# Attention over an image: the SBUF tiles of the main path moved to multiples of 128 bytes

## The chip, the cores and the metric

The kernel runs on one core of a Trainium2 chip. The metric is the device time of one execution in microseconds (us). Several executions are timed and the median is given. A profile of one execution shows when each instruction of each engine started: PE is TensorE's matmuls, PEld its weight loads, DVE is VectorE, ACT is ScalarE, POOL is GpSimd and SP is SyncE. SBUF is the on-chip memory that all of them read. A tile is a piece of it: 128 partitions, and in each partition a run of bytes at the same address. The address of a tile below is its byte address in the partition.

## The reference

For each of 4 images of 64 x 64 positions with 256 channels, with N = 4096:

```python
q = jnp.einsum('bwhc,cd->bwhd', x, Wq) + bq      # 256 -> 128
k = jnp.einsum('bwhc,cd->bwhd', x, Wk) + bk      # 256 -> 128
v = jnp.einsum('bwhc,cd->bwhd', x, Wv) + bv      # 256 -> 256
pq, pk, pv = (t.reshape(B, -1, N) for t in (q, k, v))
energy = jnp.einsum('bcn,bcm->bnm', pq, pk)
attention = jax.nn.softmax(energy, axis=-1)
out = jnp.einsum('bcm,bnm->bcn', pv, attention).reshape(B, W, H, C)
return gamma * out + x
```

All of it is float32. The energies are 4096 x 4096 for each image, with an inner dimension of 128; the second large product takes them with v.

## The kernel before

Both large products are done in `float32r`, a form of float32[...]. To keep the accuracy, each operand is split: a high part `h` of few bits, and two combinations `l` and `d` with the rest; three products, h with h, l with l and d with d, are put together to one. So there are three tiles of v that stay for an image (`vh`, `vl`, `vd`), three of the exponentials (`h`, `l`, `d`), and three forms in each `q` and `k` tile. `vh` and `vl` have two more columns, of ones: their product gives the sum of a softmax row.

The loop goes over groups of 256 columns n (16 in an image, `NG`) and in each over units of 512 m (8 in a group, `NU`). A unit has 12 energy matmuls and 24 attention matmuls:

```python
def energy(b, u, k):                                   # twice per unit, k = 0, 1
    ...
    for i in range(2):
        for to, f, first, last in ((sa, 0, True, False), (sa, 1, False, True), (sb, 2, True, True)):
            nc.tensor.matmul(
                to[:, i], kt[:, 2 * k + i, f, :], q[:, :, f, :], start=first, stop=last
            )
    ...                                                # two exponentials on ScalarE

def attend(b, u, j):                                   # twice per unit, j = 0, 1
    ...
    for out_, left, right in ((a, h, vh), (a, l, vl), (bb[:, j, :], d, vd)):
        for i in range(4):
            m = 2 * t + i // 2 + NI * (i % 2)
            nc.tensor.matmul(
                out_, left[:, i, n], right[:, m, :], ...
            )
```

The first operand, of 128 x 128, is the stationary one: it is loaded into TensorE by a weight load. The second is the moving one: it is streamed, 256 columns in the energies (two runs of 128) and in `bb`, 258 in `a`. So every matmul reads two pieces of SBUF, 512 bytes of each partition for the weights and 1024 or 1032 for the columns.

The tiles come from pools, which lie one behind the other; what is allocated first has the lowest address:

```python
    zall = const.tile([P, B * NG, NJ], F32, name="zall")
    bv4_sb = const.tile([P, KC], F32, name="bv4_sb")
    ...
        xpool, xtpool, qkv = pool("xpool", 3), pool("xtpool", 3), pool("qkv", 1)
        ppool, work, kpool = pool("ppool", 2), pool("work", 2), pool("kpool", 3)
    ...
        vh = qkv.tile([P, NM, C + 2], F32R, tag="vh", name="vh")
        vl = qkv.tile([P, NM, C + 2], F32R, tag="vl", name="vl")
        vd = qkv.tile([P, NM, C], F32R, tag="vd", name="vd")
```

`xpool` holds the tiles of x, `xtpool` the transposed ones (`xts`), `ppool` the exponentials (`x`, `y`, `h`, `l`, `d`), `work` the tiles `qks`, `v4`, `qr`, `q`, `o`, `r`, and `kpool` `f` and `k`. For each group, `load_q` fetches `qr`, `halve_q` makes the three forms `q` of it two units later, and at the group's end ScalarE copies `bb` into `o`, from which the result is made in steps during the next units (a reciprocal `r`, a scaling, four transposes, a sum with x and a store). At the very end the row sums in `zall` are tested (`ok`, `zs`, a matmul `zp`), and a second, general path is taken where they are out of range; with these inputs it isn't.

Of the kernel before, what the change touches and what calls it, by code (L numbers as in the profile page):

```python
# [9 lines left out]
F32 = mybir.dt.float32  # L10
F32R = mybir.dt.float32r
I32 = mybir.dt.int32
AF = mybir.ActivationFunctionType
ALU = mybir.AluOpType
AX = mybir.AxisListType
# [5 lines left out]
def kernel(  # L21
# [36 lines left out]
    nc = tc.nc  # L58
    B, W, H, C = x.shape
    P = 128  # L60
    N = W * H
    C2 = C // 2
    NM = N // P
    KC = C // P
    NI = NM // 2
    Z_LOW, Z_HIGH = 2.0**-60, 2.0**80
# [11 lines left out]
    const = ctx.enter_context(tc.tile_pool(name="const", bufs=1))  # L78
# [8 lines left out]
    ones = const.tile([P, P], F32, name="ones")  # L87
# [87 lines left out]
    NJ = NB // P  # L175
    NG = N // NB
    NU = NM // 4
    STEPS = NG * NU
    LOOK = 3
    E = 2.0**-12  # L180


# [4 lines left out]
    zall = const.tile([P, B * NG, NJ], F32, name="zall")  # L187
    bv4_sb = const.tile([P, KC], F32, name="bv4_sb")
    nc.scalar.mul(bv4_sb, bv_sb, 1.0 / E)

    with ExitStack() as fast:
        fast.enter_context(tc.manual_schedule())
# [3 lines left out]
        xpool, xtpool, qkv = pool("xpool", 3), pool("xtpool", 3), pool("qkv", 1)  # L196
        ppool, work, kpool = pool("ppool", 2), pool("work", 2), pool("kpool", 3)
# [3 lines left out]
        ps_t = pool("ps_t", 1, space=PSUM)  # L201


        vh = qkv.tile([P, NM, C + 2], F32R, tag="vh", name="vh")
        vl = qkv.tile([P, NM, C + 2], F32R, tag="vl", name="vl")
        vd = qkv.tile([P, NM, C], F32R, tag="vd", name="vd")
        for t in (vh, vl):
            nc.vector.tensor_copy(t[:, :, C:], ones[:, : 2 * NM].rearrange("p (m t) -> p m t", t=2))

        images, qd, kf, units, loads, now = [], {}, {}, {}, {}, {}  # L210

# [13 lines left out]
        def image(b):  # L225
# [7 lines left out]
            def v_out(i):  # L233
                now["v4"] = work.tile([P, KC, C], F32, tag="v4", name=f"v4_{b}_{i}")
                return now["v4"], bv4_sb, 1.0 / E

# [7 lines left out]
        def halved(f, x):  # L244

            h = f[:, :, 0, :]
            nc.scalar.activation(h, x, AF.Identity, scale=UPPER / 64)  # L247
            for j, s, op in ((1, -64.0, ALU.add), (2, 64.0 * (1.0 + E), ALU.subtract)):
                nc.vector.scalar_tensor_tensor(
# [12 lines left out]
        def project_v(b, i):  # L262
# [3 lines left out]
            h = vh[:, m, :C]  # L266
            nc.scalar.activation(h, v4, AF.Identity, scale=UPPER * E)  # L267

            for t, f in ((vl, 1.0 / E), (vd, 1.0 / E + 1.0)):
                nc.vector.scalar_tensor_tensor(  # L270
# [1 line left out]
                )  # L272

        def load_q(b, g):
            t = work.tile([P, NJ, P], F32, tag="qr", name=f"qr_{b}_{g}")
            nc.sync.dma_start(t, qd[b, g])
            loads[b, "qr", g] = t

# [11 lines left out]
        def energy(b, u, k):  # L290
# [10 lines left out]
# [5 lines that stand above are left out]
            for to, sp, scale in ((x, sa, (1.0 + E) / E), (y, sb, -1.0 / E)):  # L306
                nc.scalar.activation(  # L307
# [28 lines left out]
        def attend(b, u, j):  # L336
            g, t = divmod(u, NU)
            if t == j == 0:
                now["acc"] = [
                    ps_o.tile([P, C + 2], F32, tag=f"a{j}", name=f"a{j}_{b}_{g}")  # L340
                    for j in range(NJ)
                ]
                now["bb"] = ps_o.tile([P, NJ, C], F32, tag="bb", name=f"bb_{b}_{g}")
            h, l, d = units[b, u]
            a, bb = now["acc"][j], now["bb"]
            n = slice(j * P, (j + 1) * P)
# [4 lines that stand above are left out]
                    nc.tensor.matmul(  # L351
                        out_,
                        left[:, i, n],
                        right[:, m, :],
                        start=(t == i == 0 and (left is h or left is d and j == 0)),
                        stop=(t == NU - 1 and i == 3 and left is not h),
                        skip_group_check=True,
                    )
            if t == NU - 1 and j == NJ - 1:
                now["o"] = work.tile([P, NJ, C], F32, tag="o", name=f"o_{b}_{g}")  # L360
                nc.scalar.copy(now["o"], bb)

        def whole(b, g):
# [10 lines left out]

        def finish(b, g, o, xr):
            yield
            r = work.tile([P, NJ], F32, tag="r", name=f"r_{b}_{g}")
            nc.vector.reciprocal(r, zall[:, b * NG + g, :])
            nc.vector.tensor_tensor(r, r, gam.to_broadcast([P, NJ]), ALU.mult)  # L379
            for j in range(NJ):  # L380
                nc.scalar.activation(  # L381
                    o[:, j, :], o[:, j, :], AF.Identity, scale=r[:, j : j + 1]
                )
            yield
            yield
            tp = ps_t.tile([P, 2, NB], F32, tag="t", name=f"ot_{b}_{g}")
            for s in range(2):
                for j in range(NJ):
                    nc.tensor.transpose(  # L389
                        tp[:, s, j * P : (j + 1) * P], o[:, j, s * P : (s + 1) * P], ident  # L390
                    )
            yield
            nc.vector.tensor_tensor(xr, xr, tp, ALU.add)
            nc.gpsimd.dma_start(ov[b, g], xr)

        def begin(b, i):

            if i == 8:
                load_q(b, 0)
            if i == 9:  # L400
                halve_q(b, 0)
            if 8 <= i <= 10:
                load_k(b, i - 8)
            if i >= 10:
                energy(b, (i - 10) // 2, i % 2)
            if i in (12, 14):
                join(b, i // 2 - 6)
            if i in (13, 15):
                upper(b, i // 2 - 6)
                load_k(b, i // 2 - 3)  # L410

        image(0)
        for b in range(B):
# [17 lines left out]
            for u in range(STEPS):  # L431
                g, t = divmod(u, NU)
                ahead = u + LOOK
                if ahead // NU + 1 < NG and ahead % NU == 3:
                    load_q(b, ahead // NU + 1)
# [22 lines left out]
                for j in range(NJ):  # L458
                    attend(b, u, j)
                if t == NU - 1:  # L460
                    whole(b, g)
                    start(finish(b, g, now["o"], loads.pop((b, "x", g))))
# [5 lines left out]
                proceed()  # L468


    zs = const.tile([P, 1], F32, name="zs")
    zf = zall.rearrange("p n j -> p (n j)")
    ok = const.tile([P, B * NG * NJ], F32, name="ok")
    nc.vector.tensor_scalar(ok, zf, Z_LOW, None, ALU.is_ge)
    nc.vector.scalar_tensor_tensor(ok, zf, Z_HIGH, ok, ALU.is_le, ALU.mult)
    nc.vector.tensor_reduce(zs, ok, AX.X, ALU.min)
    nc.vector.tensor_scalar(zs, zs, 0.5, None, ALU.is_lt)
    with tc.tile_pool(name="ps_z", bufs=1, space=PSUM) as ps_z:
        zp = ps_z.tile([P, 1], F32, name="zp")
# [4 lines left out]
    NG = N // NB  # L484
    NJ = NB // P
    NP = NM // 2
    xg, og = columns(x, NB), columns(out, NB)
    with tc.If(nc.values_load(again[0:1, 0:1]) > 0), ExitStack() as general:
# [3 lines left out]
        xpool, xtpool, qkv = pool("gx", 2), pool("gxt", 2), pool("gqkv", 1)  # L492
        ppool, work = pool("gp", NP + 2), pool("gw", 1)
# [3 lines left out]
        for b in range(B):  # L497
# [16 lines left out]
            for g in range(NG):  # L514
                ps = []
                mx = work.tile([P, 2, NB], F32, tag="mx", name=f"gmx_{b}_{g}")
                for t in range(NP):
# [9 lines left out]
                    p = ppool.tile([P, 2, NB], F32, tag="p", name=f"gp_{b}_{g}_{t}")  # L527
# [52 lines left out]
                r = work.tile([P, NB], F32, tag="r", name=f"gr_{b}_{g}")  # L580
# [36 lines left out]
```

## Time and profile before

| | |
|---|---|
| median of 3 runs | 2519.22 us (2517.83 to 2520.44) |
| span of the profiled execution | 2518.5 us |
| mean granted TensorE clock | 0.998 |
| VectorE in a stretch of 400 us of the main loop (600 to 1000) | 332.91 us busy |
| ScalarE in the same stretch | 286.26 us busy |
| bytes moved | 498.92 MB, mean 198 GB/s |

The page counts the busy time of each engine; a busy time is a union, so instructions that overlap count once. Matmuls are pipelined: one lasts longer than the distance to the next, and the distance of their starts is what a matmul costs in a row of them. In the list of groups a line gives the source line, the engine, the output and the inputs by the program's names, the shape, the number of instructions, then busy us and the mean ns of one, then the time that the engine was idle just before them. In the timeline a line is a row of like instructions: start, duration of the whole row, and their number behind the x.

### The profile page before, as it was taken

To read this page: it belongs to the slowest core of one execution; us is meant where nothing else is said; L and a number is where in the kernel's file an instruction comes from. 1 tells how busy PE (TensorE), PEld (TensorE's weight loads), DVE (VectorE), ACT (ScalarE), POOL (GpSimd) and SP (SyncE) were. 2 spreads that over 40 slices of the span, in tenths; PEclk is the share of its full clock that TensorE was granted. 3 is DMA by queue.
4 is the path that set the end of the run, shared out by engine and by line. 5 is a ranking of instruction groups with operands and counts; after the bars stand their busy time and mean duration, and the time that the engine had idled before them with its cause. 6 is when DMAs were issued, how large, how long until landed. Compare 5 with 4: busy or idle time off the path is not lost.

```text
span 2518.5 us, 49987 instructions
## 1 busy us (share of the span) xinstructions
PE 2486.5 (99%) x19970; PEld 2440.1 (97%) x19970; DVE 2103.0 (84%) x2440; ACT 1806.3 (72%) x3138; POOL 425.3 (17%) x774
## 2 busy tenths in 40 slices
PE   8999999999999999999999999999999999999998
PEld 7999999999899999999989999999998999999998
DVE  5888888888688888888868888888886888888887
ACT  5777777777677777777667777777766777777775
POOL 3211111111411111111041111111114111111110
PEclk9999999999999999999999999999999999999999
DMA  6666666665766666666476666666647666666663
GB/s 220 204 207 206 199 200 194 211 196 156 230 214 190 209 202 201 206 192 203 139 236 210 196 200 208 198 205 197 192 144 243 209 207 192 204 200 206 199 196 101
DMA packets 137967, 498.92 MB, mean 198 GB/s; under 512 B 15872, under 2 KB 57856, under 8 KB 137728
## 3 DMA queue, kind: packets, MB, share of 16 engines
q0 software_dynamic: 92160, 453.03, 57.0%
q1 hardware_dynamic: 44032, 41.96, 5.5%
q8 instruction: 160, 2.62, 0.4%
q10 hardware_dynamic: 1536, 0.66, 0.1%
q14 instruction: 79, 0.65, 0.1%
HBM read 445.25 MB, written 50.33 MB: 197 GB/s over the span
## 4 chain that ended last, share of the span: by engine, by line
PE 91%; issue 3%; ACT 3%; DVE 2%; DMA 1%; POOL 0%; POOLq 0%; ACTq 0%; DVEq 0%
PE a L351 38%; PE bb L351 19%; PE sa L303 18%; PE sb L303 10%; PE qk L136 2%; PE v L157 2%; PE ot L389 1%; ACT v L166 1%; DMA k<-kf 1%; ACT vh L267 1%; DVE qks L145 1%; PE xt L123 0%; ACT f L247 0%; DVE vd L270 0%; DVE x L317 0%
## 5 line engine op out<-in xcount | busy, mean ns | idle before, releaser
L307 ACT ACTIVATE x<-sa 128x512 f32<-128x512 f32 x1024 | 608.8, 595 | 431.3 <-PE sa L303 422.3
L317 DVE TENSOR_TENSOR x<-x,y 128x1024 f32<-128x1024 f32 x512 | 625.1, 1221 | 165.6 <-ACT y L307 165.6
L303 PE MATMUL sa<-q,k 128*128 128x256 f32 x4096 | 744.8, 280 | 8.8 <-DMA k<-kf 4.8
L351 PE MATMUL a<-vh,h 128*128 128x258 f32 x4096 | 666.8, 285 | 0.0
L351 PE MATMUL a<-vl,l 128*128 128x258 f32 x4096 | 659.5, 283 | 1.7 <-DVE l L328 1.7
L351 PE MATMUL bb<-vd,d 128*128 128x256 f32 x4096 | 650.7, 281 | 1.8 <-DVE d L331 1.8
L303 PEld LDWEIGHTS sa<-q,k 128*128 128x128 f32 x4096 | 622.9, 188 | 10.8 <-ACT x L307 5.0
L328 DVE TENSOR_TENSOR l<-x,h 128x1024 fp32r<-128x1024 f32 x512 | 623.2, 1217 | 0.0
L331 DVE SCALAR_TENSOR_TENSOR d<-h,x 128x1024 fp32r<-128x1024 f32 x512 | 623.1, 1217 | 0.0
L307 ACT ACTIVATE y<-sb 128x512 f32<-128x512 f32 x1024 | 612.9, 599 | 0.0
L303 PE MATMUL sb<-q,k 128*128 128x256 f32 x2048 | 576.3, 281 | 0.0
L351 PEld LDWEIGHTS a<-vl,l 128*128 128x128 f32 x4096 | 563.0, 189 | 2.6 <-DVE l L328 2.6
L322 ACT ACTIVATE h<-x 128x1024 fp32r<-128x1024 f32 x512 | 543.3, 1061 | 29.1 <-DVE x L317 29.1
L351 PEld LDWEIGHTS a<-vh,h 128*128 128x128 f32 x4096 | 560.6, 190 | 1.1
L351 PEld LDWEIGHTS bb<-vd,d 128*128 128x128 f32 x4096 | 556.4, 188 | 2.6 <-issue 2.0
L287 POOL DMA_DIRECT2D k<-kf x512 | 283.6, 554 | 1487.3 <-PE sb L303 1470.5
L303 PEld LDWEIGHTS sb<-q,k 128*128 128x128 f32 x2048 | 384.5, 188 | 8.9 <-ACT y L307 1.0
L136 PE MATMUL qk<-wqk_sb,xts 128*128 128x256 f32 x512 | 124.5, 387 | 3.5 <-ACT xts L129 3.5
L157 PE MATMUL v<-xts,wv_sb 128*128 128x256 f32 x512 | 120.3, 379 | 0.0
L381 ACT ACTIVATE o<-o,r 128x256 f32<-128x256 f32 x128 | 58.3, 503 | 73.9 <-DVE r L379 73.9
L157 PEld LDWEIGHTS v<-xts,wv_sb 128*128 128x128 f32 x512 | 97.4, 190 | 13.3
L136 PEld LDWEIGHTS qk<-wqk_sb,xts 128*128 128x128 f32 x512 | 94.5, 194 | 14.7 <-ACT xts L129 3.9
(41 smaller groups left out, 876.2 us busy)
## 6 DMA issues: line engine op xcount, KB each, us to landing
k<-kf POOLq DMA_DIRECT2D x512, 768.0 KB, 4.8
x<-in_x_dram SPq DMA_DIRECT2D x128, 256.0 KB, 3.4
kf<-f POOLq DMA_DIRECT2D x64, 384.0 KB, 3.5
out_dram<-x POOLq DMA_DIRECT2D x64, 256.0 KB, 2.5
qd<-qks POOLq DMA_DIRECT2D x128, 64.0 KB, 2.2
qr<-qd SPq DMA_DIRECT2D x64, 128.0 KB, 3.1
wv_sb<-in_L_conv_Wv_dram ACTq DMA_DIRECT2D x1, 256.0 KB, 4.3
wqk_sb<-in_L_conv_Wq_dram ACTq DMA_DIRECT2D x1, 128.0 KB, 2.1
```

Of the source, the lines that this page charges most:

```text
L136: nc.tensor.matmul(qk[:, s, :], self.xt[i][:, k, s, :], wqk_sb[:, k, :], start=(k == 0), stop=(k == KC - 1),)
L145: nc.vector.tensor_tensor(dst, qk[:, :, o : o + w], bqk_sb[:, o : o + w].unsqueeze(1).to_broadcast([P, 2, w]), ALU.add,)
L157: nc.tensor.matmul(vp[:, eh, :], wv_sb[:, k, eh * P : (eh + 1) * P], self.xt[i][:, k].rearrange("p s a -> p (s a)"), start=(k == 0), stop= ...
L287: nc.gpsimd.dma_start(t.rearrange("p (i s) f d -> p i s (f d)", s=2), kf[b, u % NU])
L303: nc.tensor.matmul(to[:, i], kt[:, 2 * k + i, f, :], q[:, :, f, :], start=first, stop=last)
L307: nc.scalar.activation(to[:, 2 * k : 2 * k + 2, :], sp.rearrange("p i j d -> p i (j d)"), AF.Exp, scale=scale,)
L317: nc.vector.tensor_tensor(x, x, y, ALU.mult)
L322: nc.scalar.activation(h, units[b, u], AF.Identity, scale=UPPER)
L328: nc.vector.tensor_tensor(l, x, h.bitcast(F32), ALU.subtract)
L331: nc.vector.scalar_tensor_tensor(d, h.bitcast(F32), 1.0 + E, x, ALU.mult, ALU.subtract)
L351: nc.tensor.matmul(out_, left[:, i, n], right[:, m, :], start=(t == i == 0 and (left is h or left is d and j == 0)), stop=(t == NU - 1 and ...
L381: nc.scalar.activation(o[:, j, :], o[:, j, :], AF.Identity, scale=r[:, j : j + 1])
```

## The change

It places the tiles of the main path at addresses that are multiples of 128 bytes, and the rows of `vh` and `vl` 272 floats (1088 bytes) apart instead of 258 (1032 bytes). A filler tile of 64 bytes at the end of the constants moves what comes after it; small tiles whose size isn't a multiple of 128 bytes (`r`, `zs`, `ok`) leave the pools of the main path. The wider rows need more memory, so `qr` and `o` have one buffer instead of two. The matmuls read the same numbers of columns as before.

```diff
+    VC = C + 16
+    PAD = 16
...
+    zs = const.tile([P, 1], F32, name="zs")
+    rs = const.tile([P, 2, NJ], F32, name="rs")
+
+    const.tile([P, PAD], F32, name="pad")
...
-        vh = qkv.tile([P, NM, C + 2], F32R, tag="vh", name="vh")
-        vl = qkv.tile([P, NM, C + 2], F32R, tag="vl", name="vl")
+        vh = qkv.tile([P, NM, VC], F32R, tag="vh", name="vh")
+        vl = qkv.tile([P, NM, VC], F32R, tag="vl", name="vl")
         vd = qkv.tile([P, NM, C], F32R, tag="vd", name="vd")
         for t in (vh, vl):
-            nc.vector.tensor_copy(t[:, :, C:], ones[:, : 2 * NM].rearrange("p (m t) -> p m t", t=2))
+            nc.vector.tensor_copy(t[:, :, C : C + 2], ones[:, : 2 * NM].rearrange("p (m t) -> p m t", t=2))
...
-            t = work.tile([P, NJ, P], F32, tag="qr", name=f"qr_{b}_{g}")
+            t = work.tile([P, NJ, P], F32, tag="qr", name=f"qr_{b}_{g}", bufs=1)
...
-                        right[:, m, :],
+                        right[:, m, : out_.shape[1]],
...
-                now["o"] = work.tile([P, NJ, C], F32, tag="o", name=f"o_{b}_{g}")
+                now["o"] = work.tile([P, NJ, C], F32, tag="o", name=f"o_{b}_{g}", bufs=1)
...
-            r = work.tile([P, NJ], F32, tag="r", name=f"r_{b}_{g}")
+            r = rs[:, g % 2, :]
...
-    zs = const.tile([P, 1], F32, name="zs")
     zf = zall.rearrange("p n j -> p (n j)")
-    ok = const.tile([P, B * NG * NJ], F32, name="ok")
-    nc.vector.tensor_scalar(ok, zf, Z_LOW, None, ALU.is_ge)
...
+    with tc.tile_pool(name="check", bufs=1) as check:
+        ok = check.tile([P, B * NG * NJ], F32, name="ok")
+        nc.vector.tensor_scalar(ok, zf, Z_LOW, None, ALU.is_ge)
...
```

The addresses that the two builds assign, as the remainder by 128:

| tile | before | after |
|---|---|---|
| `ident`, `wqk_sb`, `wv_sb` | 0 | 0 |
| `x`, `xts`, `q`, `qr`, `o`, `qks`, `v4`, `x`, `y`, `h`, `l`, `d`, base of `vh`, `vl`, `vd` | 32 | 0 |
| `k`, `f` | 96 | 0 |
| rows of `vh`, `vl` | 32, 40, 48, ... (all 16 multiples of 8) | 0 and 64 in turn |
| rows of `vd` | 32 | 0 |

More of the change, by code (lines that the diff above doesn't have):

```diff
@@ L468 @@
                 proceed()
-    zs = const.tile([P, 1], F32, name="zs")
     zf = zall.rearrange("p n j -> p (n j)")
-    ok = const.tile([P, B * NG * NJ], F32, name="ok")
-    nc.vector.tensor_scalar(ok, zf, Z_LOW, None, ALU.is_ge)
-    nc.vector.scalar_tensor_tensor(ok, zf, Z_HIGH, ok, ALU.is_le, ALU.mult)
-    nc.vector.tensor_reduce(zs, ok, AX.X, ALU.min)
+    with tc.tile_pool(name="check", bufs=1) as check:
+        ok = check.tile([P, B * NG * NJ], F32, name="ok")
+        nc.vector.tensor_scalar(ok, zf, Z_LOW, None, ALU.is_ge)
+        nc.vector.scalar_tensor_tensor(ok, zf, Z_HIGH, ok, ALU.is_le, ALU.mult)
+        nc.vector.tensor_reduce(zs, ok, AX.X, ALU.min)
     nc.vector.tensor_scalar(zs, zs, 0.5, None, ALU.is_lt)
```

## The prediction

> **What bounds the kernel now.** I read four views in this order: the busy shares, the chain of work that ended last, the costliest groups, and then short stretches of the timeline of TensorE, because the first three only say which engine it is and not what sets its pace.
>
> ```profile
> PE 2486.5 (99%) x19970; PEld 2440.1 (97%) x19970; DVE 2103.0 (84%) x2440; ACT 1806.3 (72%) x3138; POOL 425.3 (17%) x774
> PEclk9999999999999999999999999999999999999999
> PE 91%; issue 3%; ACT 3%; DVE 2%; DMA 1%; POOL 0%; POOLq 0%; ACTq 0%; DVEq 0%
> L303 PE MATMUL sa<-q,k 128*128 128x256 f32 x4096 | 744.8, 280 | 8.8 <-DMA k<-kf 4.8
> L351 PE MATMUL a<-vl,l 128*128 128x258 f32 x4096 | 659.5, 283 | 1.7 <-DVE l L328 1.7
> L351 PE MATMUL bb<-vd,d 128*128 128x256 f32 x4096 | 650.7, 281 | 1.8 <-DVE d L331 1.8
> L303 PEld LDWEIGHTS sa<-q,k 128*128 128x128 f32 x4096 | 622.9, 188 | 10.8 <-ACT x L307 5.0
> ```
>
> The reader is to see three things: TensorE is busy 99% at a full clock, it carries 91% of the last chain, and its three big groups waited only 8.8, 1.7 and 1.8 us in the whole run. So nothing that feeds TensorE matters; only the pace of its own matmuls does. The means of 280 to 283 ns are lengths of overlapping instructions, not the pace. The pace is the distance between starts:
>
> ```profile
> 21.78 0.60 PE L123 MATMUL xt<-ident,x 128*128 128x128 f32 x4
> 22.22 0.60 PE L136 MATMUL qk<-wqk_sb,xts 128*128 128x256 f32 x2
> ...
> 1004.06 0.39 PE L303 MATMUL sa<-q,k 128*128 128x256 f32 x2
> 1004.29 0.28 PE L303 MATMUL sb<-q,k 128*128 128x256 f32 x1
> 1004.40 0.39 PE L303 MATMUL sa<-q,k 128*128 128x256 f32 x2
> 1004.63 0.28 PE L303 MATMUL sb<-q,k 128*128 128x256 f32 x1
> 1004.74 0.64 PE L351 MATMUL a<-vh,h 128*128 128x258 f32 x4
> 1005.22 0.64 PE L351 MATMUL a<-vl,l 128*128 128x258 f32 x4
> 1005.69 0.28 PE L351 MATMUL bb<-vd,d 128*128 128x256 f32 x1
> ```
>
> The first column is the start in us. Three energy matmuls go from 1004.06 to 1004.40, 113 ns each; four attention matmuls from 1004.74 to 1005.22, 120 ns each, though they stream nearly the same number of columns. The four transposes, whose cost is nearly all weight load, take 110 ns each (21.78 to 22.22). Taking the start-to-start distance of every record between 100 and 140 ns (longer ones are waits), the whole trace has: energies (6144) mean 115.3; attention `a` (8192, 258 columns) mean 120.6; attention `bb` (4096, 256 columns) mean 118.0; transposes 109.2.
>
> **What the Trainium skill says.** Its page "TensorE: Matmul & The Clock Gate", section "Back-to-back issue gap", gives N/2.4 + 2.5 ns between warm matmuls: 109.2 ns for 256 columns, 110.0 for 258. This trace reaches that only where nothing competes at the full rate: the fp32 projection runs at 216 ns for 256 columns at two cycles each (512/2.4 + 2.5 = 215.8), while the 18432 fp32r matmuls are 6 to 10 ns above it. The section "LDWEIGHTS (loading the stationary operand)" gives 128/1.2 = 106.7 ns; the transposes at 109.2 agree. So in the main loop weight load and matmul are equally long, and any hiccup of either is paid. The section "Step-by-step: what each phase is for" says that the two read SBUF through independent ports, so that a load steals nothing from the running matmul. The trace does not bear this out: each alone would give 109 or 110, together they give 113 to 120. Last, "SBUF — State Buffer", section "Door 1: The DMA port swizzle", has 16-byte lines, a crossing costing extra. It says nothing of 64 or 128 bytes.
>
> **The change part by part.** The instruction sequence of every engine is the same in both builds, but for names and one pair at the very end. What moves are addresses. In the build of before all the streamed and stationary tiles (`x`, `xts`, `q`, `h`, `l`, `d`, the bases of `vh`, `vl`, `vd`) begin 32 bytes past a multiple of 128, `k` and `f` 96 past; rows of `vh` and `vl` are 1032 bytes, so each begins 8 bytes further round than the last, and every odd row is only 8-aligned. In the new build all these begin on 0 of 128, and rows of `vh`, `vl` (1088 bytes) alternate between 0 and 64.
>
> *Rows.* The old kernel measures part of this by itself, as its rows pass through all sixteen positions. `a` from `vh`: even rows (16-byte aligned) 119.9 and 119.4 ns for `vh` and `vl`, odd rows 121.9 and 121.0. `bb`, whose rows are all alike, has 117.5 and 118.5 at the same places, so 1.0 of that is the place in the loop. What an 8-byte start costs is about 0.8 ns on 4096 matmuls: 3 us. And rows that already begin on 0 of 128 run at 119.8 (`vh`) and 119.3 (`vl`), no better than those at 16, 32 or 48. Alignment of the moving rows alone is thus worth almost nothing while the stationary tiles lie 32 bytes off.
>
> *Stationary tiles and q.* Here the old kernel gives no contrast, since all its fp32r weights are 32 off a multiple of 64. The excess over the floor of each kind is what can be won: energies 6144 x (115.3 - 109.2) = 37 us; `bb` 4096 x (118.0 - 109.2) = 36 us; `a` 8192 x (120.6 - 110.0) = 87 us. Sum 160 us, 6.4% of the span. It does not come from other engines: attention matmuls that ran while neither VectorE nor ScalarE was busy had the same pace (120.3 against 120.6 for `a` from `vh`, 118.1 against 117.9 for `bb`). It repeats to the nanosecond at the same place of every group, and a steady run of energies sits at 113.3 ns, which at 2.4 GHz is 272 columns' time for 256: sixteen fp32 values, 64 bytes, more than needed. That looks like one extra fetch per operand because operands straddle units of 64 bytes. I take this as the mechanism, with reserve.
>
> *Sum.* If all of it went, 2519 - 160 = 2359. I expect a part: operands of 258 columns still end 8 bytes into a new unit, and I can't tell weight from moving side. I choose two fifths, 0.4 x 160 = 64 us, as a mean of "nearly all" and "almost nothing" with somewhat more weight than half on a real gain: 2519 - 64 = 2455.
>
> *The rest.* `qr` and `o` have one buffer instead of two. A load of `q` now waits for the halving of the one before, which lies six units of 4.2 us back (25 us); the copy into `o` comes at the end of a group, and its last readers, the transposes, are done about two units into the next, so six units are free. Nothing is added. VectorE at 3.48 us busy in a unit of 4.22 us would still not be the bound at 3.9. The final test on the row sums now takes memory that the main path used, so the small `zp` matmul goes behind the last transposes; up to 2 us at the end.
>
> **Rivals.** (1) The pace is a matter of handing over between weight load and matmul, not of addresses: then only the 3 us for odd rows show and 1 or 2 us at the end take them back, 2517 to 2521. For it: rows on 0 of 128 are no faster today, and energies at some places of a group run steadily at 113.3 and at others at 117.8, with the same addresses modulo 2048, so history matters. Against it: transposes and projection keep to their floors for hundreds of matmuls. (2) Equal alignment makes it worse: if weight load and moving stream meet in the same part of memory when both start on 0 of 128, energies could go to the 117.8 of their slow places everywhere and attention to the 125 of its worst rows: 6144 x 2.5 + 12288 x 5 = 77 us more, 2596. Against it: today rows at the same position as the weights (32) run at 119.4 and 118.9, no worse than others. (3) The full gain with VectorE behind it, 2360 to 2400.
>
> **Range and chances.** A gain of 2% needs 50 us, a third of the excess. I give that 0.50; within 2% 0.41, mostly rival 1; slower 0.09, rival 2. The range 2375 to 2530 leaves out the complete gain and the worst case.
>
> **What would show it.** Right: starts of energies 109 to 111 ns apart, of `bb` 109 to 113, of `a` 110 to 116; the same idle times; ScalarE and VectorE groups unchanged in ns, with VectorE's share above 86%. If only `a` gets faster, it was the rows; if energies too, it was the stationary tiles or q. Wrong: the three distances as before, or a pattern that only moved to other places of the group.

## The result and the profile after

The changed kernel takes 2548.91 us (median of 4 runs, 2548.18 to 2549.81) against 2519.39 us: 1.0118 times as long, with a 95% interval of 1.0100 to 1.0135. It is slower by 29.5 us.

The page of the changed kernel, the lines that answer to those shown of before (busy shares, the chain, groups with busy us and mean ns):

```profile
PE 2513.1 (99%) x19970; PEld 2470.3 (97%) x19970; DVE 2103.8 (83%) x2440; ACT 1801.3 (71%) x3138; POOL 424.8 (17%) x774
PE 93%; ACT 2%; DVE 2%; issue 1%; DMA 1%; POOL 0%; ACTq 0%; POOLq 0%; DVEq 0%
L309 PE MATMUL sa<-q,k 128*128 128x256 f32 x4096 | 769.0, 285 | 6.5 <-ACT x L313 3.9
L357 PE MATMUL a<-vl,l 128*128 128x258 f32 x4096 | 661.7, 283 | 1.7 <-DVE l L334 1.7
L357 PE MATMUL bb<-vd,d 128*128 128x256 f32 x4096 | 656.6, 282 | 1.8 <-DVE d L337 1.8
```

TensorE is still busy 99%, its waits are the same few us, and the two engines that read and write the moved tiles have nearly the same busy time (VectorE 2103.8 us after 2103.0, ScalarE 1801.3 after 1806.3). What grew is the busy time of TensorE itself, and in it above all the energies `sa`: 769.0 after 744.8 us. The starts in its timeline show how:

```profile
1001.17 0.40 PE L309 MATMUL sa<-q,k 128*128 128x256 f32 x2
1001.41 0.28 PE L309 MATMUL sb<-q,k 128*128 128x256 f32 x1
1001.53 0.40 PE L309 MATMUL sa<-q,k 128*128 128x256 f32 x2
...
1001.89 0.40 PE L309 MATMUL sa<-q,k 128*128 128x256 f32 x2
...
1002.25 0.40 PE L309 MATMUL sa<-q,k 128*128 128x256 f32 x2
```

Three energies now go by every 0.36 us, 120 ns each, where before there were stretches of 0.34 us: of all distances between energies 61% were 115 ns or less, and now it is 0.6%. Over the whole trace (the means are of distances from 100 to 140 ns, as in the prediction; the sums are of all distances, waits included, so they can fall where the mean stays):

| matmuls | mean before | mean after | sum of all distances, before and after, us |
|---|---|---|---|
| energies (6144) | 115.3 ns | 119.6 ns | 736.1, 758.3 (+22.2) |
| `bb` (4096) | 118.0 | 119.6 | 484.8, 492.9 (+8.1) |
| `a` (8192) | 120.6 | 120.5 | 997.5, 994.3 (-3.2) |
| transposes of x | 109.2 | 109.2 | 36.8, 35.4 (-1.4) |

One more piece is at the end. In the timeline of the changed kernel the last store and the test of the row sums stand so:

```profile
2535.14 0.70 POOL L400 DMA_DIRECT2D out_dram<-x  x1 [26.20 <-DVE x L399]
2537.78 0.23 DVE L480 TENSOR_SCALAR ok<-zall 128x128 f32<-128x128 f32 x1 [2.94 <-DMA out_dram<-x]
2538.98 0.56 PE L486 MATMUL zp<-zs,ones 128*128 128x1 f32 x2 [4.87 <-DVE zs L483]
2539.58 0.16 DVE L487 CAST again<-zp 128x1 int32<-128x1 f32 x1 [0.74 <-PE zp L486]
```

The reader is to see the bracket of `ok`: VectorE waited 2.94 us until the store had landed. In the kernel before, the same test was over before the last transposes. (`ok` did not have to leave the constants for the alignment: its 512 bytes are a multiple of 128.) From the last transpose to the end of the span it is 13.8 us now (2533.8 to 2547.7), and was 9.2 (2509.3 to 2518.5): 4.6 us more.

The sum: 22.2 + 8.1 - 3.2 - 1.4 + 4.6 = 30.3 us, against spans of 2518.5 and 2547.7, which differ by 29.2.

### The profile page after: what moved, and what is told of

The parts are those of the page before. It is cut to its first block, busy times and chain, and to the rows that moved or that the text cites. A ratio compares the mean times of both kernels' runs of the same rounds, so it can differ in the third digit from the quotient of the medians.

```text
span 2547.7 us, 49989 instructions
## 1 busy us (share of the span) xinstructions
PE 2513.1 (99%) x19970; PEld 2470.3 (97%) x19970; DVE 2103.8 (83%) x2440; ACT 1801.3 (71%) x3138; POOL 424.8 (17%) x774
## 3 DMA queue, kind: packets, MB, share of 16 engines
q10 hardware_dynamic: 1536, 0.66, 0.1%
## 4 chain that ended last, share of the span: by engine, by line
PE 93%; ACT 2%; DVE 2%; issue 1%; DMA 1%; POOL 0%; ACTq 0%; POOLq 0%; DVEq 0%
PE a L357 39%; PE bb L357 19%; PE sa L309 19%; PE sb L309 10%; PE qk L136 3%; PE v L157 2%; PE ot L395 1%; ACT v L166 1%; PE xt L123 1%; ACT vh L273 1%; DVE qks L145 1%; DMA k<-kf 1%; DVE vd L276 0%; ACT f L253 0%; DVE x L323 0%
## 5 line engine op out<-in xcount | busy, mean ns | idle before, releaser
L309 PE MATMUL sa<-q,k 128*128 128x256 f32 x4096 | 769.0, 285 | 6.5 <-ACT x L313 3.9
L309 PEld LDWEIGHTS sa<-q,k 128*128 128x128 f32 x4096 | 637.1, 191 | 8.4 <-ACT x L313 4.7
L309 PE MATMUL sb<-q,k 128*128 128x256 f32 x2048 | 585.8, 286 | 0.0
L328 ACT ACTIVATE h<-x 128x1024 fp32r<-128x1024 f32 x512 | 543.4, 1061 | 29.2 <-DVE x L323 29.2
L309 PEld LDWEIGHTS sb<-q,k 128*128 128x128 f32 x2048 | 391.0, 191 | 6.4 <-ACT y L313 1.0
L157 PE MATMUL v<-xts,wv_sb 128*128 128x256 f32 x512 | 120.7, 380 | 0.0
L387 ACT ACTIVATE o<-o,rs 128x256 f32<-128x256 f32 x128 | 58.3, 502 | 73.9 <-DVE rs L385 73.9
```

The costliest lines, as they stand in the source:

```text
L157: nc.tensor.matmul(vp[:, eh, :], wv_sb[:, k, eh * P : (eh + 1) * P], self.xt[i][:, k].rearrange("p s a -> p (s a)"), start=(k == 0), stop= ...
L309: nc.tensor.matmul(to[:, i], kt[:, 2 * k + i, f, :], q[:, :, f, :], start=first, stop=last)
L328: nc.scalar.activation(h, units[b, u], AF.Identity, scale=UPPER)
L387: nc.scalar.activation(o[:, j, :], o[:, j, :], AF.Identity, scale=r[:, j : j + 1])
```

## The experiments

Three theories were set against each other. *Distance*: the pace is set by where the moving columns start relative to where the weights start, modulo 128 bytes. *Absolute*: a start on 0 of 128 is slow by itself. *Hand-over*: addresses do not matter, only the history of the sequence.

**A grid of positions.** A kernel that leaves out everything but matmuls (it computes no attention): series of 24 fp32r matmuls, 256 columns, weights starting at `ow` and columns at `om` of 128, other rows and weights each time in steps that are multiples of 128 bytes.

```python
for i in range(count):
    s = ow // 4 + (i % 8) * 128
    m = om // 4 + (i % 8) * 256
    nc.tensor.matmul(p[:, :n], w[:, s : s + P], v[:, m : m + n], start=True, stop=True)
```

> Only matmuls, in rows of 24 with one pair of start positions each (weights at a, moving columns at b, both modulo 128 bytes), nothing else running. Distance theory (what counts is b - a): the start-to-start distance has the same value along each diagonal of the grid, near 120 ns where b - a = 0 and 113 ns or less where it is 64. Absolute theory (a start on 0 of 128 is slow by itself): a = b = 0 is slow and the other points of that row and column are too, whatever the difference. Hand-over theory (addresses don't matter, history does): all points alike. Weight loads alone (32 columns): 109 ns at every position if a load by itself does not mind its start.

Start-to-start distance in ns, mean of the last 16 of each series; rows: start of the weights, columns: start of the columns (the first series began before the full clock was granted, with 213 ns a matmul; its value is from the next kernel of this kind, at the same positions):

```
weights\columns   0     16     32     48     64     80     96    112
  0             120.0  118.6  116.7  118.4  117.8  120.0  120.2  113.3
 16             118.3  118.3  120.0  118.2  116.7  118.3  118.1  120.0
 32             118.4  117.4  120.0  118.6  116.7  118.3  117.8  120.0
 48             123.3  120.0  118.3  118.3  120.0  118.2  116.6  118.3
 64             117.8  119.2  118.3  117.1  120.0  118.6  116.7  118.3
 80             118.6  113.3  123.4  120.0  118.4  118.3  120.0  118.2
 96             117.3  118.9  113.4  119.1  118.3  116.9  120.0  118.6
112             120.0  117.9  118.7  113.3  123.3  120.0  118.4  118.4
```

Each pair is written weights/columns. The values run along the diagonals: 120.0 at 0/0, 32/32, 64/64, 96/96, and 118.3 or 118.4 at 16/16, 48/48, 80/80, 112/112; 116.7 at 0/32, 32/64 and 64/96. Position 0 of 128 is not slow: 0/112 has the best value, 113.3. So the absolute theory falls. Expected was 113 or less at a distance of 64. Columns 64 further gave 117.8 to 118.3; 64 less gave 113.3 in three of four places and 117.8 in the fourth. Distance is right as the kind of the rule, and the rule is not as simple as "64 is good". The timeline of three series with the weights on 96 and the columns on 0, 32 and 96 (start, duration of the 24):

```profile
156.06 2.98 PE L60 MATMUL wgma<-v,w 128*128 128x256 f32 x24
161.74 2.90 PE L60 MATMUL wgmc<-v,w 128*128 128x256 f32 x24
172.99 3.04 PE L60 MATMUL wgmg<-v,w 128*128 128x256 f32 x24
```

The second is the pair that the energies of the kernel before had (`k` on 96, `q` on 32): 2.90 us, 113.4 ns a matmul. The third is equal positions: 3.04 us. But the energies read their columns in two runs of 128, and the same pair in that form took 117.8 ns in the same run (equal positions: 119.6 to 120.0). So the old pair has two paces, as the kernel of before has. Nor are all cells of the table fixed: 48/0, 123.3 here, took 117.9 and 118.3 in two later kernels of this kind behind other series. Series of 32 columns, with weights on 0, had a load every 111.6 ns; at the other positions the granted clock had dropped to 0.5, so they say nothing.

**Moving k alone, in both directions, and both operands apart.** In the changed kernel, a filler of 64 bytes ahead of `f` and `k`:

```diff
+        kpool.tile([P, 16], F32, tag="kpad", name="kpad", bufs=1)
```

> The changed kernel with k moved from 0 to 64 of 128, q left at 0. Distance theory: energies go from 120 to 113 ns apart, 6144 x 6.5 = 40 us less, about 2509 us. Absolute theory: q still starts on 0, energies stay near 120, within 10 us of 2549. Hand-over theory: 2549.

2536.27 us, 1.0059 (1.0042 to 1.0076) times before: 12.6 us less than the changed kernel, with energies at 116.5 ns on the mean, and nothing else moved (`a` 120.5, `bb` 119.5). The expected 113 comes in only a part of the units. Two units of its timeline:

```profile
1002.70 0.39 PE L310 MATMUL sa<-q,k 128*128 128x256 f32 x2
1003.04 0.39 PE L310 MATMUL sa<-q,k 128*128 128x256 f32 x2
1003.38 0.39 PE L310 MATMUL sa<-q,k 128*128 128x256 f32 x2
...
1006.96 0.40 PE L310 MATMUL sa<-q,k 128*128 128x256 f32 x2
1007.31 0.40 PE L310 MATMUL sa<-q,k 128*128 128x256 f32 x2
1007.66 0.40 PE L310 MATMUL sa<-q,k 128*128 128x256 f32 x2
```

The first unit goes by in steps of 0.34 us for three, the next in 0.35 (113.3 and 117.8 ns each), with the same positions modulo 128. So at this distance there are two paces. In both units the first three energies took 0.36 us; the pace after that held to the unit's end.

The same filler in the kernel of before puts `k` from 96 on 32, where `q` lies:

> The kernel of before with k moved from 96 to 32 of 128, where q lies as well. Distance theory: energies go from a mean of 115.3 to about 120 ns, 6144 x 4.7 = 29 us more, about 2548 us. Absolute theory: neither operand is on 0 of 128, nothing changes, 2519 us. Hand-over theory: 2519 us or a shift of a few us in either direction.

2538.05 us, 1.0068 (1.0051 to 1.0085): 17 us more than the runs of before beside it, energies 119.0. One filler of 64 bytes takes more than half of the loss in the old kernel, where nothing lies on 0 of 128. That again speaks against the absolute theory and against hand-over alone.

Then v's tiles and `k` on 64, `q`, `h`, `l`, `d` on 0, in the changed kernel (the filler of the constants moved ahead of the pool of `h`, `l`, `d`, and one more ahead of `k`):

```diff
-    const.tile([P, PAD], F32, name="pad")
...
+        kpool.tile([P, 16], F32, tag="kpad", name="kpad", bufs=1)
+        ppool.tile([P, 16], F32, tag="ppad", name="ppad", bufs=1)
```

> The changed kernel with the differences set to 64 where they can be: vd at 64 and d at 0, k at 64 and q at 0; rows of vh and vl alternate between 64 and 0 against h and l at 0. Distance theory: energies 113 ns, bb from 119.7 to about 113, half of the rows of a to about 114: 40 + 27 + 8192/2 x 6 = 25, so 2549 - 92 = 2457 us. Absolute theory: h, l, d, q still on 0, at most a few us. Hand-over theory: 2549 us.

2524.30 us, 1.0014 (1.0007 to 1.0021): 25 us of the 29.5 are gone, with `bb` at 117.8 and energies at 116.1. The gain of 92 us that the simple rule promised did not come.

**Rows and positions taken apart.** First the wider rows and single buffers with all tiles on their old positions:

```diff
-    PAD = 16
+    PAD = 24
...
+        kpool.tile([P, 16], F32, tag="kpad", name="kpad", bufs=1)
```

> The changed kernel (272-float rows, single qr and o) with all tiles back at the old positions, 32 and k at 96. Distance theory: energies and bb as before (115.3, 118.0), a between 119.5 and 120.5; 2519 us within 8. Theory that the wider rows or the single buffers cost the time: 2540 us or more.

Then the new positions with the old rows:

```diff
-    VC = C + 16
+    VC = C + 2
```

> The changed kernel with rows of 258 floats as before, everything else on 0 of 128. Distance theory: energies near 120, bb near 119.7 as in the changed kernel, a 120.5; 2550 us within 6. Theory that the wider rows or single buffers cost the time: 2519 us within 8.

| positions | rows | us | energies | `bb` | `a` |
|---|---|---|---|---|---|
| old | 258 | 2519.4 | 115.3 | 118.0 | 120.6 |
| old | 272 | 2533.65, ratio 1.0044 (1.0027 to 1.0061) | 116.7 | 119.5 | 120.5 |
| new | 258 | 2548.91, ratio 1.0106 (1.0089 to 1.0123) | 119.6 | 118.2 | 120.7 |
| new | 272 | 2548.91, ratio 1.0118 (1.0100 to 1.0135) | 119.6 | 119.6 | 120.5 |

(That the last two medians agree is chance: against the runs of before beside each, 2522.51 and 2519.39 us, the differences are 26.4 and 29.5 us.)

The energies follow the positions, `bb` follows the rows, in both pairs of kernels. The first of the two runs missed its expectation by more than its margin: 272-float rows with single `qr` and `o` cost 11 us against the runs of before beside it (2522.51), though no tile of the energies or of `bb` had changed its position modulo 128. The late end, 4.6 us, is part of it. Between the traces, whose spans differ by 15.0 us (2518.5 and 2533.5), the energies are 5.3 us and `bb` 7.4 us longer. `bb` has equal positions for weights and columns in all four kernels and still has two paces, so its pair alone does not set it. Rows of `vh` and `vl` are read just before both. This fits a part of the hand-over theory: the pace with which a row of matmuls starts comes from the matmuls ahead of it. For the energies that is argued; a row of bare matmuls below shows it for one pair.

**Is TensorE alone with it?** A kernel that leaves out all other engines and runs only the matmul sequence of the units, at chosen positions, 8 units for each of 54 settings (`kb`, `qb`, `wb`, `vb`: start positions in bytes; `st_`: row distance in floats):

```python
kt = K + 1536 * (u % 3) + kb // 4                  # energies: weights and two runs of columns
s, m = kt + (2 * k + i) * 384 + f * 128, Q + qb // 4 + f * 128
...
hb = W + 1024 * (u % 3) + wb // 4                  # attention; l and d alike
s, m = hb + i * 256 + j * 128, V + vb // 4 + (2 * u + i // 2 + 16 * (i % 2)) * st_
```

> The matmul sequence of the kernel's units (12 energies, 24 attention matmuls, same buffers, row order and shapes) without any other engine, for 54 settings of start positions and row distances, 8 units each. Distance theory: the settings of before, of the changed kernel, and of the runs with k moved give the means of those kernels within 1 ns (energies 115, 119.5, 116.5, 119; bb 118, 119.7, 119.5, 118), so nothing but positions is needed; among the others some lie below 115 in energies and below 118 in attention. Theory that ScalarE, VectorE or the transfers take part: the settings all agree with each other and with none of the kernels.

Means in ns, without the first 24 of a setting's 288 matmuls:

| positions | bare sequence: energies, `a` of vh, of vl, `bb` | kernel |
|---|---|---|
| of before | 114.7, 120.3, 120.0, 118.4 | 115.3, 120.9, 120.2, 118.0 |
| of the changed kernel | 119.8, 121.2, 120.8, 119.8 | 119.6, 120.1, 120.9, 119.6 |
| changed, `k` on 64 | 116.2, 121.2, 120.2, 119.7 | 116.5, 120.1, 120.9, 119.5 |
| before, `k` on 32 | 120.0, 120.6, 120.1, 118.3 | 119.0, 120.6, 120.2, 118.0 |
| v and `k` on 64, rest 0 | 115.7, 120.3, 120.4, 117.7 | 116.1, 120.4, 119.9, 117.8 |

With nothing but matmuls running, the kernels' means come back within 1.1 ns, in every line. So the slower pace needs no other engine and no transfer; what is left for waits is the late end.

**What the surplus is made of.** Matmuls alone again, at first with 512 columns, with fewer weight columns, with other numbers of columns, and with one pair of positions behind different predecessors:

```python
series(f"cols{..}", 0, 16 * b, n=512, cols=cols)   # cols = 128, 64, 32 weight columns
series(f"n{..}", 0, 0, n=n, step=512)              # n = 256, 320, 384, 448, 512
series(f"lock{..}", 64, 0, count=40)               # behind 20, 25 and 31 other matmuls
```

> Only matmuls, in rows with one pair of start positions each. With 512 moving columns the weight load (112 ns) is hidden behind 213 ns of streaming; in the grid such matmuls still took 227 to 233 ns. Shared-read theory (each weight load takes read turns from the moving stream): the surplus over 213.3 ns shrinks with the number of weight columns, from about 14 ns for 128 to 7 for 64 and 3.5 for 32, is the same for 256 to 512 moving columns, and depends on the difference of the start positions. Hand-over theory (a fixed cost of changing weights): the same surplus for 128, 64 and 32 weight columns, and for every difference. For 256 columns with weights at 64 and columns at 0 the pace is 113.3 or 117.8 ns depending on what ran before, if it is a matter of phase; always one of them, if positions alone decide.

```profile
271.09 3.04 PE L60 MATMUL na<-v,w 128*128 128x256 f32 x24
283.82 4.32 PE L60 MATMUL nc<-v,w 128*128 128x384 f32 x24
...
315.46 4.88 PE L60 MATMUL locka<-v,w 128*128 128x256 f32 x40
327.97 4.72 PE L60 MATMUL lockb<-v,w 128*128 128x256 f32 x40
341.02 4.73 PE L60 MATMUL lockc<-v,w 128*128 128x256 f32 x40
```

The first two lines are equal positions with 256 and 384 columns: 120.0 and 173.3 ns a matmul by their starts, so 53.3 ns for 128 columns (0.417 each), and a surplus of 120.0 - 256 x 0.417 = 13.3 ns that is the same for both. It is the same at 320 columns (146.6) and at 512 (226.6), but 20.0 at 448 (206.7). With 512 columns (213.3 ns of streaming) the series of this run and of the grid had means of 226.6 to 234.8 ns, 13 to 21 ns above, though a weight load has twice the time. The three last lines are weights on 64 and columns on 0: 117.8 ns in the first, 113.3 in the other two, each with 40 matmuls and different matmuls ahead. The expectation of a surplus that halves with the weight columns failed: 226.9 ns for 128 weight columns, 229.7 for 64, 231.6 for 32 at equal positions, and no common order at the three other pairs. So it is not read turns taken for each weight column.

Then the same piece of SBUF every time (`step=0` for the columns, `wstep=0` for the weights), and few weight columns (`half`: 64, `tiny`: 32):

> Rows of 48 matmuls of 256 columns in which the weights, the columns or both are the same piece of SBUF every time, or only 64 or 32 weight columns are loaded. If the surplus over 106.7 ns comes from two reads meeting in the same places, it depends on the start positions also with both fixed (120 at distance 0, 113 to 118 at others), and shrinks with fewer weight columns. If it is a cost of each change from one matmul to the next, it stays at 6.7 or 13.3 ns with 32 weight columns. If it came from jumps of the moving address, it vanishes when the same columns are streamed again.

```profile
26.63 5.92 PE L60 MATMUL botha<-v,w 128*128 128x256 f32 x48
43.91 5.92 PE L60 MATMUL fixa<-v,w 128*128 128x256 f32 x48
49.67 5.61 PE L60 MATMUL halfa<-v,w 128*64 128x256 f32 x48
...
60.56 5.60 PE L60 MATMUL bothb<-v,w 128*128 128x256 f32 x48
76.88 5.60 PE L60 MATMUL fixb<-v,w 128*128 128x256 f32 x48
...
115.61 5.82 PE L60 MATMUL halfc<-v,w 128*64 128x256 f32 x48
121.26 5.92 PE L60 MATMUL tinyc<-v,w 128*32 128x256 f32 x48
```

`a` is both on 0, `b` weights on 64 and columns on 0, `c` weights on 0 and columns on 32. Reading the same weights and the same columns 48 times (`fix`) gives the same time as walking through SBUF (`both`): 5.92 and 5.92, 5.60 and 5.60 us. So in these rows neither jumps of the address nor the larger place in SBUF matters. With 32 weight columns five of the six pairs tried run at 113.3 or 113.4 ns, equal positions among them, but `c` is slower (120.0) than with 128 (116.6). So the load has a part in it, and a cost proportional to what is loaded is ruled out. What remains is a cost per matmul of 6.7 to 16.7 ns at 256 columns, set by the start positions and the sequence ahead. What in the chip makes it was not found.

One assumption of all these tables, that only the remainder by 128 counts, does not hold. The same kernel has rows at weights 0 with the columns moving on by 1024, 1152 or 1536 bytes each time, so that all start on 0 of 128:

```profile
227.26 5.92 PE L60 MATMUL stepa<-v,w 128*128 128x256 f32 x48
284.11 5.76 PE L60 MATMUL stepf<-v,w 128*128 128x256 f32 x48
306.77 5.92 PE L60 MATMUL steph<-v,w 128*128 128x256 f32 x48
```

The first and third take 120 ns each time. The second, whose columns start on 0 and 128 of 256 in turn, alternates between some 113 and 121 ns, with a mean of 116.6; a step of 1280 bytes, a multiple of 256, gave 120.0 again. So positions have to be told at least modulo 256. By its build the changed kernel has `k`, `q`, `h`, `l`, `d` and `vd` all on 128 of 256, so its equal positions are equal in this sense too; in the old kernel with `k` on 32, `k` and `q` are 128 apart, and its energies (119.0 where the bare sequence had 120.0) are the worst fit of the energies in the table above.

**The end.** Rows of 258 floats, and the test's tile among the constants again:

```diff
-    with tc.tile_pool(name="check", bufs=1) as check:
-        ok = check.tile([P, B * NG * NJ], F32, name="ok")
+    ok = const.tile([P, B * NG * NJ], F32, name="ok")
```

> The changed kernel with rows of 258 floats (the run before showed that this alone changes nothing) and with the tile of the final test in memory of its own again, as before. If the test waits for the last store only because its tile lies on a tile of the main path: 4 to 5 us less than 2548.9, so 2544. Rival, that the end is set by the last store whatever the test does: 2549.

2542.57 us, 1.0091 (1.0074 to 1.0108): 6 us less than the same kernel with the late test, or 3 us when each is set against the runs of before beside it. Its `zp` starts at 2529.60, ahead of the last transposes at 2531.03, as in the kernel before, and from the last transpose to the end it is 9.2 us again, 4.6 less. That the tile's memory makes the test late is shown; that it is late because it lies on a tile of `x`, as expected, is not (see the run with v and `k` on 64 again, below).

**Looking for something better.** 125 settings of the bare sequence, with start positions and row distances drawn at random, separately for `vh`, `vl` and `vd`:

> The unit's matmul sequence alone, for 125 settings of start positions and row distances drawn at random around the better ones of the map, the first two being the positions of before, the fifth those of the changed kernel. Distance theory: before takes about 4.21 us a unit and the changed kernel 4.32 (12 x 119.8 + 16 x 121 + 8 x 119.8 ns); rows 288 floats apart with v's and q's tiles 64 bytes further than the weights (the third setting) 4.15; the best of the others below 4.12. Theory that no arrangement does better in a sequence like this: the best setting is within 1% of before.

The positions of before took 4247 ns a unit, those of the changed kernel 4332, the largest but for the first series, which began before the full clock was granted. The best had rows 288 floats apart with all columns on 64 and all weights on 0: 4187. The expected 4120 did not appear. To try this in the kernel, rows of 288 floats need 4096 bytes, which `qks` and `v4` gave up; and a twin has the same 64-byte filler in another place, so that everything starts on 0:

```diff
-    const.tile([P, PAD], F32, name="pad")
...
+        ppool.tile([P, PAD], F32, tag="pad", name="pad", bufs=1)
```

> The changed kernel with rows of vh and vl 288 floats apart (1152 bytes, so every row has the same remainder by 128), and the 64-byte filler between q's pool and the pool of h, l, d: everything that is streamed (q, vh, vl, vd) starts on 64 of 128, all weights (k, h, l, d) on 0. To pay for the rows, qks has one buffer and v4 shares o's two; the tile of the last test lies where nothing is pending. Distance theory, from the bare sequence with these positions (energies 113.3, a 117.8 and 121.2, bb 114.3; 4187 ns a unit against 4247 for before): up to 512 x 60 ns = 31 us below before, 2488 to 2502 us, energies at 113.3 in every unit. If only history and not positions counted: 2519 or more.

> The same kernel with the same 64-byte filler moved to the end of the constants: streamed tiles and weights all start on 0 of 128, nothing else differs. Distance theory, from the bare sequence with these positions (energies 120.0, a 121.7 and 120.4, bb 119.6; 4334 ns a unit): slower than before, 2540 to 2563 us, and at least 45 us slower than its twin with the filler in the other place. If rows, buffers or order of pools made the difference: the two within 10 us.

2549.14 us, 1.0112 (1.0095 to 1.0129), and 2573.46 us, 1.0209 (1.0192 to 1.0226). The two kernels differ in nothing but the place of 64 bytes, and by 24 us: positions alone, shown in the kernel itself. It is half of the 45 expected, and the first is no gain at all: most of its energies ran at 117 to 119 ns (mean 117.4, 9% of them at 115 or less), where the bare sequence had 113.3, and `bb` at 118.0 where it had 114.3. Yet its pace is not what makes it 28 us slower than before: with `a` at 119.4 the three means come to 6144 x 2.1 - 8192 x 1.2 = 3 us more. The rest is mostly waits and the clock: the projections (`qk`, `v` and the transposes of x) take 13.7 us more from start to start, the test is late here too, and the granted clock was 0.5 for 17 us of the loop (3.4 us in the kernel before). The single `qks` costs, as the waits of the first show, which the kernel before does not have:

```profile
DVE qks L145 <- DMA qd<-qks: 26.9, 19, 3.2
PEld v L157 <- DVE qks L145: 9.3, 10, 3.0
```

(us waited in total, times, longest us.) Why the pace of the bare setting did not come is open. The sequence ahead is one reason that fits; another, not tried, is that the two agree only modulo 128: the build of this kernel puts `k` and `d` on 128 and `q` and `vd` on 64 of 256, the bare setting had 0 and 64. (The bare sequence of the map with weights on 64 and columns on 0 had `bb` at 119.3 and energies at 113.4, so this could account for `bb` and hardly for the energies.) A good setting of the bare sequence need not be one of the kernel. Two smaller ones, which give up no further buffers. First the positions of the run with v and `k` on 64, with the test's tile behind an unused one:

```diff
+        check.tile([P, 3200], F32, name="gap")
         ok = check.tile([P, B * NG * NJ], F32, name="ok")
```

> The changed kernel with v's tiles and k on 64 of 128 and q, h, l, d on 0 (as in the run with both moved, 2524 us), and the tile of the last test in memory where nothing is pending. The tail was worth 4 to 6 us when it was mended alone: 2519 us, level with before. Rival, that the tail is hidden with these positions: 2524.

2523.60 us, 1.0012 (1.0005 to 1.0018). The test had been moved only inside memory that the main path gives back at the end, and still waited for the last store (its first instruction at 2511.08, 2.94 us of waiting). So this run does not say what the end is worth with these positions, but it says something else: by the build, `ok` lay on `x` in the changed kernel and lies on `vh` here, and the wait is the same. So an overlap with the tile that is being stored is not what it takes. In both kernels `ok` lies in memory given back; in those where it has its own, the one of before and the run above, the test did not wait. Then rows of 260 floats, `vh` on 32, `vl` and `vd` on 16, `k` on 64, the rest on 0:

```diff
-    VC = C + 16
+    VC = C + 4
...
+        v16 = qkv.tile([P, 28 + NM * (VC + C)], F32R, tag="vl", name="vl")[:, 28:]
+        vl = v16[:, : NM * VC].rearrange("p (m c) -> p m c", m=NM)
+        vd = v16[:, NM * VC :].rearrange("p (m c) -> p m c", m=NM)
```

> The changed kernel with rows of 260 floats, vh starting on 32, vl and vd on 16, k on 64 and q, h, l, d on 0, and the last test out of the way: the best setting of the bare sequence that fits in memory without giving up buffers (4223 ns a unit against 4247 for before). Distance theory as the bare sequence has it: up to 12 us below before, 2507 to 2519. If the phase that the sequence falls into in the real kernel differs from the bare one, as in the run with all columns 64 bytes off: 2519 to 2535.

2521.09 us, 1.0001 (0.9992 to 1.0009), in the second of the two ranges: energies 115.5, `a` 120.2 and 118.8, `bb` 118.7, and the late end. With the test among the constants:

> The run with rows of 260 floats again, with the tile of the last test among the constants (the two runs that only shifted it inside the freed memory still waited for the last store, at 2511 of 2521 us in the one with v and k moved). Its test then runs before the last store, as in the kernel of before: 5 us less than 2521.1, so 2516, about 0.2% below before. Rival: 2521, if the end is set by the last store.

2517.20 us, 0.9984 (0.9977 to 0.9991): 4 us below the runs of before beside it (2521.3). It is the only version that is faster than before, and hardly worth its trouble.

## Why the prediction was wrong

**What bounds the kernel** was right: TensorE's pace and nothing else. The bare sequence shows it.

**The rows** were right in their main point: rows that start on 0 of 128 bring `a` nothing (120.6 to 120.5). What the step left out is what follows them: with the rows changed and the positions kept, `bb` and the energies rose by 1.5 and 1.4 ns.

**Stationary tiles and q** is the step that failed. The text took as the mechanism "one extra fetch per operand because operands straddle units of 64 bytes", so an aligned operand would lose it, and the sum took 0.4 x 160 us from it (2455 us, 64 below before). Aligned, `a` lost nothing, the energies went from 115.3 up to 119.6 ns, and the kernel took 2548.9 us. In the grid, operands that straddle nothing (0/0) have one of the larger surpluses, 13.3 ns, and a straddling pair (96/32) one of the smallest, 6.7. The surplus belongs to the pair of positions and to the sequence, not to one operand. Before, `k` on 96 and `q` on 32 happened to be a good pair, at 115 ns or less in 61% of the energies; on 0 of 128 the pair became a poor one, 0.6%. Moving `k` alone by 64 bytes showed it both ways: 12.6 us back in the changed kernel, 17 us lost in the old one. The 160 us that could be won were too many as well: no settled row of fp32r matmuls came below 113.3 ns, so against the floors of 109.2 and 110.0 at least 18432 x 4.1 = 76 us of them (an estimate from the rows tried) were never there. The profile of before had no second pair for the energies, and the text said so; but the observation that it set against the mechanism, rows on 0 being no faster, was right and was given too little weight.

**Rival 2** (equal alignment makes it worse) got 0.09 and came true in direction, though at 1.2% slower the result lies in the class within 2% (0.41), which the text gave mostly to rival 1. Its size was 77 us; for the energies it had 2.5 ns and they rose by 4.3, for attention 5 ns and it rose by 0.5 on the mean of 12288 (119.7 to 120.2). Its counter-argument, that rows on the weights' position were no slower, held for attention and not for the energies. **Rival 1**'s sign, that the same addresses show two paces, was real too: 113.3 and 117.8 at one pair. Its core, that addresses do not matter, fell.

**The rest**: the single `qr` and `o` cost nothing that the waits show. The end was put at "up to 2 us"; it measured 4.6. The prediction saw that `zp` goes behind the transposes, and not that the test before it waits for the last store to land.

## What to carry to other kernels

An alignment rule is a hypothesis about pairs of operands: before padding everything to one multiple, measure the bare instruction at several pairs of positions, over 256 bytes at least, which takes one run of a few hundred us. Where the pace of a stream of matmuls shows small jumps that repeat at the same place of a loop, look at positions and sequence before looking at other engines, and test a setting in the kernel itself, as the sequence ahead decides with them. A tile put into memory that the main path has just given back can wait for work that never touches it: 2.94 us here, for a store from another tile.

## What the runs showed of the hardware that was not expected

An fp32r matmul with its own weight load never came at 256 columns to the estimate of 109.2 ns that the prediction worked out from the Trainium skill ("TensorE: Matmul & The Clock Gate", "Back-to-back issue gap"): settled series lay between 113.3 and 123.4 ns, with 0.417 ns a column plus a surplus. The section gives that formula for an isolated matmul and says that in a stream of loads and matmuls both set the spacing, which the prediction left out; the traces agree with that sentence, since fewer weight columns changed the pace, and not with its figure of about 131 ns for 512 columns in such a stream: here it was 226.6 or more. The steady values 113.3, 120.0, 206.7, 226.7 and 233.3 (at 256, 448 and 512 columns) lie one, two or three times 6.67 ns above the streaming time, 6.67 being what 16 columns take. The surplus remains at 512 columns, where there are 226.6 ns from load to load and a row of 32 columns had a load every 111.6.
